# A graph-attention kernel whose first block gathers 27 columns instead of 38, with the edges left over fetched by one gather

## The chip, the cores and the metric

One core of one Trainium2 chip runs the whole kernel. The metric is the device time of one execution in microseconds (us). The kernel before takes 3907.3 us, the median of three runs (3907.01 to 3914.32).

## The reference

Three graph-attention layers over one graph of 6250 nodes, 100,000 edges and 256 features per node, all in float32. Edges are sorted by target. Cut to what matters:

```python
def gatv2(x, src, dst, Wl, Wr, att, b):          # 4 heads of 64, twice; self loops added
    xl, xr = (x @ Wl).reshape(n, 4, 64), (x @ Wr).reshape(n, 4, 64)
    e = leaky_relu(xl[src] + xr[dst], 0.2)
    logits = einsum('ehc,hc->eh', e, att)
    ex = exp(logits - segment_max(logits, dst)[dst])
    alpha = ex / segment_sum(ex, dst)[dst]
    return segment_sum(xl[src] * alpha[:, :, None], dst) + b

h = gatv2(elu(gatv2(x, ..., loops)), ..., loops)
x = layernorm(x + h)
# last layer: 8 heads of 32, no self loops
Wh = einsum('nf,hfd->hnd', x, W)
e = leaky_relu(s1[:, src] + s2[:, dst], 0.2)     # s1, s2: products of Wh with a
attn = softmax of e over the edges of each target
x = layernorm(x + segment_sum(attn * Wh[:, src], dst))
```

## The kernel before, in words

**Plan.** `make_plan` (0 to about 152 us) counts the edges of every node, puts the nodes in the order of their degrees, most edges first, and writes for every node a row with the numbers of its sources (`near_d`). The sorted nodes form 49 blocks of 128, one node to a partition. `columns()` fixes at build time, from the statistics of such a graph, how many source columns each block gets: 38, 25, 24, 23, 22, 21, 21, 20 and so on down to 9, together 814. Where the drawn graph does not fit these numbers, `fits` is zero and a general path of the kernel is taken instead. A node with fewer edges than its block has columns gets the number of an extra row ("nobody") in the places left over; its values make the softmax weight zero.

**Layers 0 and 1** (`layer2`, about 153 to 1492 and 1493 to 2728 us). For each block, `gather_rows` (L1207) issues one indirect DMA per column from GpSimd (POOL): 128 rows of about 1 KB, one to a partition, from a table in HBM (`xl_d`). The rows land in tiles `g` of up to nine columns; the pool `rows` has nine such tiles for all blocks. `row_tiles` and `chunks` cut a block into tiles of even size: with the node's own row as a further column, block 0 has 39 columns in five tiles, block 1 has 26 in three.

Each engine works in the order of the program, written by hand (`manual_schedule`). For block b the order is: load of block b+3 (`start`), gathers of block b+1, products for the own rows of block b+1 (`ready`), then `attend(b)`: on VectorE (DVE), tile by tile, `z` = max (L1396), `z` times the attention vector (L1397) and the sum per head into `lg` (L1398); the maximum `top` (L1272); on ScalarE (ACT) the exponentials `wt` with their sums `den` (L1279). Then `end(b-1)` on DVE: `h` = `acc` times `den` (L1415), and what follows from it. Then `weighted_sum(b)`: DVE multiplies the rows by their weights (L1309), ACT does so for a few of the last columns (L1308), and TensorE (PE) adds up the columns in PSUM, one product with the identity per column (L1316, `acc`). The next thing on DVE is the `z` of block b+1, while PE adds up the columns of block b. A tile of `rows` is free for a later gather when PE has read its columns.

In layer 0 the source numbers of blocks 0 to 2 are also sorted (`sort_sources`), so that 14, 12 and 11 of their gathers can be issued at the end of the layer before (`begin`, EARLY), ahead of the last four blocks of that layer's output.

**Last layer** (about 2729 to 3904 us). Gathers of blocks from `whs_d` without an own column (block 0: 38 columns in five tiles), the logits on DVE (L1567, L1571), exponentials on ACT (L1289), the weighted rows into one product tile `prod` of 27 columns (L1327) and their sum (L1336), all on DVE; PE has no part in it. The output is scattered by one indirect DMA per block (L1597).

Of the kernel before, what the change touches and what calls it, by code (L numbers as in the profile page):

```python
# [45 lines left out]
def columns(E, N, NB):  # L46

    mean = E / N
    pmf = [math.exp(-mean)]
    for k in range(1, 200):
        pmf.append(pmf[-1] * mean / k)
    over, sd = [], []
    for c in range(199):
        p = sum(pmf[c + 1 :])
        g = sum((k - mean) * pmf[k] for k in range(c + 1, 200))
        over.append(N * p)
        sd.append(math.sqrt(max(N * (p * (1.0 - p) - g * g / mean), 0.0)))  # L60
    cols = []
    for b in range(NB):
        most = P * b
        cols.append(next(
            c for c in range(199) if (over[c] + 3.5 * sd[c] <= most if b else over[c] < 0.01)
        ))
    low = max((c for c in range(199) if N - over[c] <= P // 4), default=0)
    high = next(c for c in range(199) if over[c] <= P // 4)
    return cols, low, high


@with_exitstack
# [565 lines left out]
@with_exitstack  # L638
def kernel(
    ctx: ExitStack,  # L640
    tc: tile.TileContext,
    x: bass.AP,
    src: bass.AP,
    dst: bass.AP,
    wl1: bass.AP,
    wr1: bass.AP,
    att1: bass.AP,
    b1: bass.AP,
    wl2: bass.AP,
    wr2: bass.AP,  # L650
    att2: bass.AP,
    b2: bass.AP,
    w3: bass.AP,
    a3: bass.AP,
    out: bass.AP,
):
    nc = tc.nc
    N, F = x.shape
    E = src.shape[0]
    NB = -(-N // P)  # L660
    NP = NB * P
    cols, low, high = columns(E, N, NB)
    CM = max(cols)
    H2, D2 = att1.shape
    H1 = w3.shape[0]
    W2 = H2 * (D2 + 1)

    dram = ctx.enter_context(tc.tile_pool(name="plan_dram", bufs=1, space=DRAM))
    plan = ctx.enter_context(tc.tile_pool(name="plan", bufs=1))
    node_i = plan.tile([P, NB], I32, name="node_i")  # L670
    fits = plan.tile([P, 1], I32, name="fits")
    done = plan.tile([P, 1], I32, name="done")
    ident = plan.tile([P, P], F32, name="ident")
    eps = plan.tile([P, 1], F32, name="eps")
    nobody = plan.tile([1, 2, max(W2 + 1, F + H1)], F32, name="nobody")
    att = [plan.tile([P, H2, D2 + 1], F32, name=f"att_r{i}") for i in range(2)]
    wc = [plan.tile([P, 2, 2, H2, D2 + 1], F32, name=f"wcat{i}") for i in range(2)]
    wh = plan.tile([P, 2, F + 2 * H1], F32, name="wh_cat")
    fixed = plan.tile([P, 4, F], F32, name="fixed_r")
    xl1_d = dram.tile([NP + 1, W2 + 1], F32, name="xl1_d")  # L680
    near_d = dram.tile([NP, CM + F], F32, name="near_d")

    with tc.manual_schedule():
        make_plan(
            tc, x, src, dst, ((wl1, wr1, att1), (wl2, wr2, att2)), (b1, b2), w3, a3,
            cols, low, high, node_i, fits, ident, eps, nobody, att, wc, wh, fixed, xl1_d, near_d,
        )
        nc.vector.memset(done, 0)

    att = [t.rearrange("p h d -> p (h d)") for t in att]  # L690
    wc = [w.rearrange("p j c h d -> p j c (h d)") for w in wc]
    ok = nc.values_load(fits[0:1, 0:1], min_val=0, max_val=1)
    with tc.If(ok != 0):
        with tc.manual_schedule():
            tile_by_degree(
                tc, x, att1, b1, b2, w3, a3, out, cols, node_i, near_d, ident, eps, nobody,
                xl1_d, att, wc, wh, fixed, done,
            )
    right = nc.values_load(done[0:1, 0:1], min_val=0, max_val=1)
    with tc.If(right == 0):  # L700
        tile_general_path(
            tc, x, src, dst, wl1, wr1, att1, b1, wl2, wr2, att2, b2, w3, a3, out,
        )
# [1 line left out]

@with_exitstack
def make_plan(
    ctx, tc, x, src, dst, layers, biases, w3, a3, cols, low, high, node_i, fits, ident, eps, nobody,
    att, wc, wh, fixed, xl1_d, near_d,
):  # L710

# [382 lines left out]
    nc.vector.tensor_scalar(  # L1094
        wrong[:, KE + NB :], upto[:, NB - 1 :], float(E), None, op0=OP.not_equal
    )
    bad = one.tile([P, 1], F32, name="bad")
    nc.vector.reduce_sum(bad, wrong, axis=AX.X)
    tables(4)
    pb = ps.tile([P, 1], F32, name="pb", tag="ph")  # L1100
    nc.tensor.matmul(pb, ones, bad, start=True, stop=True)
    nc.vector.tensor_scalar(fits, pb, 0.0, None, op0=OP.is_equal)
    right(0)
    left(1, nc.vector)
    right(1)
# [23 lines left out]
def tile_by_degree(  # L1129
# [9 lines left out]
    T = 9  # L1139
    A1 = F + H1  # L1140
    W2 = H2 * (D2 + 1)
    CM = max(cols)

    dram = ctx.enter_context(tc.tile_pool(name="deg_dram", bufs=1, space=DRAM))
    consts = ctx.enter_context(tc.tile_pool(name="deg_consts", bufs=1))
# [4 lines left out]
    def per_head(t, H):  # L1150
# [9 lines left out]


    AHEAD = (NB - LATE) * P
    KEY = CM.bit_length()
    assert (NP + 1) << KEY < 1 << 24
    CK = -(-CM // 8) * 8
    number = consts.tile([P, CK], F32, name="number")
    nc.gpsimd.iota(number, pattern=[[1, CK]], base=0, channel_multiplier=0,
                   allow_small_or_imprecise_dtypes=True)
    soon = consts.tile([P, len(EARLY), max(EARLY)], I32, name="soon")
    late = consts.tile([P, len(EARLY)], F32, name="late")  # L1170
    ones = consts.tile([P, P], F32, name="ones_l")
# [30 lines left out]
    def gather_rows(b, rows, cut, own, table, of, width, j0, j1):  # L1202


        for g, (s0, s1) in zip(rows, cut):
            for j in range(max(s0 - own, j0), min(s1 - own, j1)):
                nc.gpsimd.indirect_dma_start(  # L1207
                    out=g[:, j + own - s0, :width], out_offset=None, in_=table,
                    in_offset=source(of, b, j),
                )  # L1210

    def row_tiles(b, own):
        cut = chunks(cols[b] + own)
# [51 lines left out]
        cut = [n * i // k for i in range(k + 1)]  # L1265
        return list(zip(cut, cut[1:]))

    def weights(work, ps, lg, S, H, scalar=0):


        top = work.tile([P, H], F32, name="top")
        nc.vector.tensor_reduce(  # L1272
            top, lg[:, :S, :].rearrange("p s h -> p h s"), axis=AX.X, op=OP.max, negate=True
# [3 lines left out]
        if H <= 4:  # L1277
            for h in range(H):
                nc.scalar.activation(  # L1279
                    wt[:, :, h], lg[:, :S, h], AF.Exp, bias=top[:, h : h + 1],  # L1280
                    accum_out=den[:, h : h + 1],
                )
            by = None
            if scalar:
                by = work.tile([P, scalar, H], F32, name="by")
                nc.scalar.copy(by, wt[:, S - scalar :, :])
            return (wt, by), lambda: den
        nc.vector.tensor_add(lg[:, :S, :], lg[:, :S, :], top[:, None, :].to_broadcast([P, S, H]))
        nc.scalar.activation(wt, lg[:, :S, :], AF.Exp)  # L1289
# [4 lines left out]

        return (wt, None), add_up

    def weighted_sum(ps, rows, cut, wts, H, width, between):

        wt, by = wts
        acc = ps.tile([P, F], F32, name="acc")  # L1300
# [1 line left out]
        for g, (s0, s1) in zip(rows, cut):  # L1302
# [10 lines left out]
            if s0 == 0:  # L1313
                between()
            for t in range(n):
                nc.tensor.matmul(acc, ident, g4[:, t], start=s0 + t == 0, stop=s0 + t == S - 1)  # L1316
        return acc

    def added_up(work, prod, rows, cut, wts, H, width, between):
# [40 lines left out]
    def layer2(i, table, of, width, start, own, finish, follow):  # L1360
# [5 lines left out]
        with ExitStack() as es:  # L1366
# [9 lines left out]
            def gather(b):  # L1376
                first = EARLY[b] if b in begun else 0
                rows, cut = begun.pop(b) if first else row_tiles(b, 1)
                gather_rows(b, rows, cut, 1, table, of, width, first, cols[b])
                state[b] = [rows, cut]  # L1380

            later = []
# [6 lines left out]
            def attend(b):  # L1389
# [3 lines left out]
                for g, (s0, s1) in zip(rows, cut):  # L1393
# [4 lines left out]
                    nc.vector.reduce_sum(  # L1398
                        lg[:, s0:s1, :], z.rearrange("p t (h d) -> p t h d", h=H2), axis=AX.X
                    )  # L1400
                few = min(S // 3, cut[-1][1] - cut[-1][0] - 1) if b + 1 < NB else 0
                wt, new = weights(work, ps, lg, S, H2, few)
                while later:
                    later.pop()()
                if i == 0:
# [17 lines left out]
            for b in range(3):  # L1423
                if (i, b) not in loaded:
                    start(b)
            gather(0)
            ready(0)
            later.pop()()
# [3 lines left out]
            for b in range(NB):  # L1432
# [19 lines left out]
                    if b:  # L1452
                        last.append(rest())

                acc = weighted_sum(ps1, rows, cut, wt, H2, D2 + 1, between)
                if i == 0 and b + 1 < NB:
                    none(state[b + 1][2])
                if last:
# [92 lines left out]
    with ExitStack() as es:  # L1551
# [4 lines left out]
        def gather(b):  # L1556
            first = EARLY[b] if b in begun else 0
            rows, cut = begun.pop(b) if first else row_tiles(b, 0)
            gather_rows(b, rows, cut, 0, wh_d[:, :], spots, A1, first, cols[b])
            state[b] = (rows, cut)  # L1560

        def attend(b):
            rows, cut = state.pop(b)
            S = cols[b]
            lg = work.tile([P, CM, H1], F32, name="lg", bufs=2)
            for g, (s0, s1) in zip(rows, cut):
                nc.vector.tensor_add(  # L1567
                    lg[:, s0:s1, :], g[:, : s1 - s0, F:A1],
                    s2[:, b : b + 1, :].to_broadcast([P, s1 - s0, H1]),
                )  # L1570
# [3 lines left out]
            return rows, cut, *weights(work, ps, lg, S, H1)  # L1574

        def end(b, acc, den):
            h = work.tile([P, F], F32, name="h")
            nc.vector.tensor_mul(
                per_head(h, H1), per_head(acc, H1), den.unsqueeze(2).to_broadcast([P, H1, D1])
            )  # L1580
# [8 lines left out]
            return rest  # L1589

        gap = work.tile([P, 1], F32, name="gap", bufs=1)
        prod = work.tile([P, 3 * T, F], F32, name="weighted", bufs=1)

        def put_out(b, y, apart):
            if apart:
# [10 lines left out]
        for b in range(NB):  # L1606
# [12 lines left out]
                    puts[b - 1] = rest()  # L1619

            acc = added_up(work, prod, rows, cut, wt, H1, D1, between)
        puts[NB - 1] = end(NB - 1, acc, den)()
        for b in sorted(puts):
            put_out(*puts[b], apart=True)
# [28 lines left out]
```

## Time and profile before

| what | value |
|---|---|
| median of 3 runs | 3907.3 us (3907.01 to 3914.32) |
| the profiled execution | 3906.24 us; its span in the trace 3904.4 us |
| mean granted TensorE clock | 0.669 |
| DVE busy | 2859.7 us (73%) |
| POOL busy | 2558.8 us (66%) |
| PE busy | 1465.1 us (38%) |
| ACT busy | 1093.2 us (28%) |
| gathers per layer | 814, 0.95 us (layers 0 and 1) and 1.03 us (last layer) each |

The busy tenths of the page cut the span into 40 slices of 97.6 us. A row of the costliest groups has the line, the engine, the operation, the tiles written and read, the count, the busy time and the mean of one in ns, and then the idle time just before and what ended most of it. A row of the waits names who waited, for what, the total in us, how often and the longest. A line of the timeline has its start, its duration and, in brackets, the idle time before it.

### The profile page before, as it was taken

Reading aid. Unit: us, or ns where it says so; the run is one execution under the profiler, and the core shown is the slowest. Engines: PE = TensorE matmul, PEld = TensorE weight load, DVE = VectorE, ACT = ScalarE, POOL = GpSimd, SP = SyncE. Lnnn points to the kernel's source line nnn. Section 1 sums busy time; section 2 is a strip of 40 time slices with the busy share of each in tenths; the row PEclk is TensorE's granted clock in tenths of the full one; section 3 lists DMA queues with packets and bytes.
Section 4 is the critical chain, followed back from the end, with each engine's and each line's share of the span. In section 5 each row is a group of like instructions: output and inputs, shape, how many; then the busy total and the mean of one; then the engine's idle time right before and its main releaser. Section 6 shows DMA issues by size and latency. Waiting matters only on the chain.

```text
span 3904.4 us, 23669 instructions
## 1 busy us (share of the span) xinstructions
PE 1465.1 (38%) x5147; PEld 1100.0 (28%) x5147; DVE 2859.7 (73%) x2624; ACT 1093.2 (28%) x4179; POOL 2558.8 (66%) x2642
## 2 busy tenths in 40 slices
PE   5335655646667653355545455554000000000000
PEld 4223443435455542243433334442000000000000
DVE  6267888768888867798877889895686666666655
ACT  2123433434445441243334334442000000000000
POOL 6466666666666654666666666663777777777774
PEclk8667787777888886676766777776555555555555
DMA  8443333333334333333434344342433333333332
GB/s 192 101 94 100 104 103 100 105 102 103 105 103 107 104 102 71 103 106 105 112 104 111 107 110 111 109 111 69 100 107 105 97 96 97 97 97 96 97 97 56
DMA packets 197563, 399.62 MB, mean 102 GB/s; under 512 B 63516, under 2 KB 115994, under 8 KB 197396
## 3 DMA queue, kind: packets, MB, share of 16 engines
q0 software_dynamic: 123488, 342.06, 33.7%
q1 hardware_dynamic: 66226, 54.22, 4.9%
q10 hardware_dynamic: 7698, 1.74, 0.4%
q8 instruction: 45, 0.74, 0.1%
q14 instruction: 106, 0.87, 0.1%
HBM read 357.84 MB, written 40.42 MB: 102 GB/s over the span
## 4 chain that ended last, share of the span: by engine, by line
issue 24%; POOL 21%; PE 16%; DVE 14%; another core or an unknown queue 12%; ACT 9%; DMA 2%; DVEq 0%; SPq 0%; ACTq 0%; POOLq 0%
POOL g L1207 19%; PE acc L1316 10%; ACT g L1308 4%; PE pm L1261 3%; DVE z L1397 3%; DVE z L1396 3%; DVE lg L1398 3%; ACT wt L1279 2%; DVE weighted L1327 1%; DVE g L1309 1%; DMA g<-xl_d,near_r 1%; POOL out L1597 1%; ACT xT L1256 1%; PE pl L1261 1%
## 5 line engine op out<-in xcount | busy, mean ns | idle before, releaser
L1207 POOL DMA_INDIRECT g<-xl_d,near_r x1591 | 1508.6, 948 | 843.6 <-issue 455.7
L1316 PE MATMUL acc<-g,ident 128*128 128x256 f32 x3452 | 1015.0, 455 | 910.1 <-issue 361.4
L1316 PEld LDWEIGHTS acc<-g,ident 128*128 128x128 f32 x3452 | 768.0, 229 | 1152.9 <-issue 617.4
L1207 POOL DMA_INDIRECT g<-whs_d,near_r x777 | 802.2, 1032 | 293.9 <-issue 251.9
L1308 ACT ACTIVATE g<-g,by 128x64 f32<-128x64 f32 x2064 | 550.4, 337 | 331.3 <-issue 328.0
L1396 DVE TENSOR_TENSOR z<-g,pr 128x1820 f32<-128x1820 f32 (+4 forms) x236 | 503.4, 2133 | 39.3 <-DMA g<-xl_d,near_r 25.7
L1397 DVE TENSOR_TENSOR z<-z,at 128x1820 f32<-128x1820 f32 (+4 forms) x236 | 503.7, 2134 | 8.1
L1398 DVE TENSOR_REDUCE lg<-z 128x28 f32<-128x1820 f32 (+4 forms) x236 | 503.6, 2134 | 8.1
L1336 DVE TENSOR_REDUCE acc_v<-weighted 128x256 f32<-128x4096 f32 (+16 forms) x49 | 349.2, 7127 | 11.7 <-remote 6.1
L1309 DVE TENSOR_TENSOR g<-g,wt 128x1792 f32<-128x1792 f32 (+5 forms) x236 | 353.8, 1516 | 2.9
L1567 DVE TENSOR_TENSOR lg<-g,s_r 128x56 f32<-128x56 f32 (+4 forms) x113 | 22.8, 214 | 367.4 <-DMA g<-whs_d,near_r 300.0
L1289 ACT ACTIVATE wt<-lg 128x128 f32<-128x128 f32 (+17 forms) x49 | 14.0, 285 | 901.2 <-DVE top L1272 309.9
L1256 ACT COPY xT<-pt 128x256 f32<-128x256 f32 x147 | 55.0, 374 | 704.8 <-remote 367.3
L1327 DVE TENSOR_TENSOR weighted<-g,wt 128x1792 f32<-128x1792 f32 (+4 forms) x113 | 229.5, 2048 | 0.0
L1447 DVE RECIPROCAL den<-den 128x4 f32<-128x4 f32 x98 | 17.4, 177 | 226.8 <-ACT wt L1279 158.9
L1279 ACT ACTIVATE wt<-lg,top 128x19 f32<-128x19 f32 (+14 forms) x392 | 116.1, 296 | 209.0 <-DVE top L1272 83.7
L1415 DVE TENSOR_TENSOR h<-acc,den 128x256 f32<-128x256 f32 x98 | 40.7, 416 | 166.8 <-remote 122.3
L1261 PE MATMUL pm<-wh_cat,xT 128*128 128x272 f32 x196 | 83.9, 568 | 192.7 <-issue 108.7
L1261 PE MATMUL pm<-wcat,xT 128*128 128x260 f32 x392 | 138.5, 512 | 45.8 <-ACT xT L1256 44.8
L1261 PEld LDWEIGHTS pm<-wcat,xT 128*128 128x128 f32 x392 | 96.9, 261 | 82.1 <-ACT xT L1256 61.7
L1261 PEld LDWEIGHTS pm<-wh_cat,xT 128*128 128x128 f32 x196 | 46.0, 260 | 213.5 <-issue 113.5
L1597 POOL DMA_INDIRECT out<-y,node_i x49 | 50.3, 1027 | 49.6 <-ACT y L1358 35.6
(180 smaller groups left out, 1511.1 us busy)
## 6 DMA issues: line engine op xcount, KB each, us to landing
g<-xl_d,near_r POOLq DMA_INDIRECT x1591
g<-whs_d,near_r POOLq DMA_INDIRECT x777
whs_d<-row SPq DMA_DIRECT2D x49, 132.0 KB
xl_d<-xl SPq DMA_DIRECT2D x49, 130.0 KB
xl_d<-row SPq DMA_DIRECT2D x49, 130.0 KB
xr_d<-row SPq DMA_DIRECT2D x49, 130.0 KB
two<-xl_d SPq DMA_DIRECT2D x49, 130.0 KB
two<-xr_d SPq DMA_DIRECT2D x49, 130.0 KB
```

What stands on the lines that cost most here:

```text
L1207: nc.gpsimd.indirect_dma_start(out=g[:, j + own - s0, :width], out_offset=None, in_=table, in_offset=source(of, b, j),)
L1256: nc.scalar.copy(xT, pt)
L1261: nc.tensor.matmul(pm, xT[:, c, :], w[:, c, :], start=c == 0, stop=c == 1)
L1279: nc.scalar.activation(wt[:, :, h], lg[:, :S, h], AF.Exp, bias=top[:, h : h + 1], accum_out=den[:, h : h + 1],)
L1308: nc.scalar.mul(g4[:, t, h, :], g4[:, t, h, :], by[:, t - m, h : h + 1])
L1309: nc.vector.tensor_mul(g4[:, :m], g4[:, :m], wt[:, s0 : s0 + m, :].unsqueeze(3).to_broadcast([P, m, H, F // H]),)
L1316: nc.tensor.matmul(acc, ident, g4[:, t], start=s0 + t == 0, stop=s0 + t == S - 1)
L1327: nc.vector.tensor_mul(prod[:, s0 - base : s1 - base, :].rearrange("p t (h d) -> p t h d", h=H), g[:, :n, :F].rearrange("p t (h d) -> p t ...
L1336: nc.vector.reduce_sum(part, prod[:, : s1 - base, :].rearrange("p s f -> p f s"), axis=AX.X)
L1396: nc.vector.tensor_max(z, g[:, :n, :W2], xr[:, None, :].to_broadcast([P, n, W2]))
L1397: nc.vector.tensor_mul(z, z, at[:, None, :].to_broadcast([P, n, W2]))
L1398: nc.vector.reduce_sum(lg[:, s0:s1, :], z.rearrange("p t (h d) -> p t h d", h=H2), axis=AX.X)
```

## The change

Block 0 gets `held` = 27 columns instead of 38. Its nodes with more than 27 edges have "other" edges; `held` is chosen such that their number over the block is at most 128 (by the same statistics; the plan counts them and otherwise takes the general path). `find_few` gives each of them a partition, once, at the beginning of layer 0: `node_of` and `edges_of` are 0/1 matrices between nodes and edges, `hot` marks which of its node's other edges an edge is, `few_at` is its source number. In each layer `gather_few` fetches the rows of all of them with one gather, after the gathers of block 0. In layers 0 and 1 their logits are worked out edge by edge (the node's own values come to the edges by a product with `node_of`), and go to their nodes by a product with `edges_of` (`few_logits`); `top`, `wt` and `den` then cover 27 + 1 + 11 places. `few_sum` takes the weights back to the edges by a product with `node_of`, multiplies the rows, and adds them to the nodes with a product with `edges_of`, into the same `acc` as the columns and after them. In the last layer the same two functions work on a PSUM tile of their own, added to `acc_v`. The sort of sources has 32 keys instead of 40, `h` of the last layer has two buffers instead of three and `prod` 24 columns instead of 27.

```diff
@@ columns
+    pmf += [0.0] * 200
+    held = next(
+        c for c in range(199)
+        if N * sum((k - c) * pmf[k] for k in range(c, 200))
+        + 3.5 * math.sqrt(N * sum((k - c) ** 2 * pmf[k] for k in range(c, 200))) <= P
+    )
@@ make_plan
+    nc.vector.tensor_scalar(
+        bad[:, 1:], got[:, 2, :1], -float(held), 0.0, op0=OP.add, op1=OP.max
+    )
...
-    nc.vector.tensor_scalar(fits, pb, 0.0, None, op0=OP.is_equal)
+    many = one.tile([P, 1], F32, name="many")
+    nc.vector.tensor_scalar(many, pb[:, 1:], float(P), None, op0=OP.is_gt)
+    nc.vector.tensor_add(many, many, pb[:, :1])
+    nc.vector.tensor_scalar(fits, many, 0.0, None, op0=OP.is_equal)
@@ tile_by_degree (called with [held] + cols[1:])
+    CM = near_d.shape[1] - F
+    FEW = CM - cols[0]
...
+    def find_few(work, ps):
+        got = work.tile([P, 1 + FEW], F32, name="few_got", bufs=1)
+        nc.vector.tensor_copy(got[:, 1:], sources[:, 0, cols[0] :])
+        nc.vector.tensor_single_scalar(lack, got[:, 1:], float(NP), op=OP.is_lt)
...
+        po = ps.tile([P, 1], F32, name="few_o", tag="tp")
+        nc.tensor.matmul(po, edges_of, n[:, :1], start=True, stop=True)
...
+        pk = ps.tile([P, 1 + FEW], F32, name="few_k", tag="tp")
+        nc.tensor.matmul(pk, node_of, got, start=True, stop=True)
...
+        nc.vector.tensor_copy(few_at[:, :1], which)
+        pe = ps.tile([P, P], F32, name="few_e", tag="tp")
+        nc.tensor.transpose(pe, node_of, ident)
+        nc.scalar.copy(edges_of, pe)
+
+    def gather_few(table, j, width):
+        nc.gpsimd.indirect_dma_start(
+            out=few_row[:, :width], out_offset=None, in_=table,
+            in_offset=bass.IndirectOffsetOnAxis(ap=few_at[:, j : j + 1], axis=0),
+        )
+
+    def few_logits(work, ps, lg, few, H):
+        each = work.tile([P, FEW, H], F32, name="few_each", bufs=1)
+        nc.vector.tensor_mul(each, few (broadcast), hot (broadcast))
+        pf = ps.tile([P, FEW, H], F32, name="few_lg", tag="tp")
+        nc.tensor.matmul(pf, edges_of, each, start=True, stop=True)
+        nc.vector.tensor_add(lg[the FEW places], pf, lack (broadcast))
+
+    def few_sum(work, ps, acc, wt, S, H, width, first):
+        share = work.tile([P, FEW, H], F32, name="few_each", bufs=1)
+        nc.scalar.copy(share, wt[:, S : S + FEW, :])
+        pw = ps.tile([P, FEW, H], F32, name="few_w", tag="tp")
+        nc.tensor.matmul(pw, node_of, share, start=True, stop=True)
+        each = work.tile([P, FEW, H], F32, name="few_weight", bufs=1)
+        nc.vector.tensor_mul(each, pw, hot (broadcast))
+        weight = work.tile([P, H], F32, name="few_wt", bufs=1)
+        nc.vector.reduce_sum(weight, each, axis=AX.X)
+        part = work.tile([P, F], F32, name="few_part", bufs=1)
+        nc.vector.tensor_mul(part, few_row, weight (broadcast))
+        nc.tensor.matmul(acc, edges_of, part, start=first, stop=True)
@@ weighted_sum
             for t in range(n):
-                nc.tensor.matmul(acc, ident, g4[:, t], start=s0 + t == 0, stop=s0 + t == S - 1)
+                nc.tensor.matmul(
+                    acc, ident, g4[:, t], start=s0 + t == 0, stop=s0 + t == S - 1 and not more
+                )
+        if more:
+            more(acc, wt, S)
         return acc
@@ layer2, gather
                 gather_rows(b, rows, cut, 1, table, of, width, first, cols[b])
+                if b == 0:
+                    gather_few(table, i, width)
@@ layer2, attend, after the tiles' z
+                if b == 0:
+                    own_r = work.tile([P, W2], F32, name="few_own", bufs=1)
+                    nc.scalar.copy(own_r, xr)
+                    po = pst.tile([P, W2], F32, name="few_r", tag="tp")
+                    nc.tensor.matmul(po, node_of, own_r, start=True, stop=True)
+                    none(po)
+                    z = zp.tile([P, T, W2], F32, name="z")[:, 0, :]
+                    nc.vector.tensor_max(z, few_row[:, :W2], po)
+                    nc.vector.tensor_mul(z, z, at)
+                    few_lg = work.tile([P, H2], F32, name="few_lg", bufs=1)
+                    nc.vector.reduce_sum(few_lg, per_head(z, H2), axis=AX.X)
+                    few_logits(work, pst, lg, few_lg, H2)
+                    if i == 0:
+                        nc.vector.tensor_copy(few_at[:, 1:], few_row[:, W2 : W2 + 1])
@@ layer2, before gather(0)
+            if i == 0:
+                find_few(work, pst)
@@ layer2, per block
-                acc = weighted_sum(ps1, rows, cut, wt, H2, D2 + 1, between)
+                acc = weighted_sum(
+                    ps1, rows, cut, wt, H2, D2 + 1, between,
+                    b == 0 and (lambda acc, wt, S: few_sum(
+                        work, pst, acc, wt, S, H2, D2 + 1, False)),
+                )
@@ last layer
+            if b == 0:
+                gather_few(wh_d[:, :], 1, A1)
...
+            if b == 0:
+                few_logits(work, ps, lg, few_row[:, F:A1], H1)
+                nc.vector.tensor_add(lg[the FEW places], lg[the FEW places], s2 of block 0 (broadcast))
...
-        prod = work.tile([P, 3 * T, F], F32, name="weighted", bufs=1)
+        prod = work.tile([P, 24, F], F32, name="weighted", bufs=1)
...
             acc = added_up(work, prod, rows, cut, wt, H1, D1, between)
+            if b == 0:
+                more = ps.tile([P, F], F32, name="few_acc", tag="tp")
+                few_sum(work, ps, more, wt[0], cols[0], H1, D1, True)
+                nc.vector.tensor_add(acc, acc, more)
```

Views of tiles are shortened in the diff: "(broadcast)" stands for the repetition over heads or places.

## The prediction
> **What bounds the kernel now.** I read the page first: busy tenths, then the costliest groups, then the waits, then the timelines of the stretches that the change touches.
>
> ```profile
> PE   5335655646667653355545455554000000000000
> DVE  6267888768888867798877889895686666666655
> POOL 6466666666666654666666666663777777777774
> ...
> L1207 POOL DMA_INDIRECT g<-xl_d,near_r x1591 | 1508.6, 948 | 843.6 <-issue 455.7
> L1316 PE MATMUL acc<-g,ident 128*128 128x256 f32 x3452 | 1015.0, 455 | 910.1 <-issue 361.4
> ...
> L1207 POOL DMA_INDIRECT g<-whs_d,near_r x777 | 802.2, 1032 | 293.9 <-issue 251.9
> ```
>
> No engine is full, but POOL is level all through: it issues one gather per column and does nothing else. A gather is busy 0.948 us and, in the timeline, comes 0.30 us after the last: a pitch of 1.25 us. In the last layer, issues and output scatters (797 from 2771 to 3857) follow without a stall, 1.363 us apart: that layer is POOL's. In layers 0 and 1 POOL stalls once a block:
>
> ```profile
> POOL g L1207 <- remote: 151.2, 43, 6.1
> ...
> DVE h L1415 <- remote: 122.3, 11, 27.0
> ...
> POOL g L1207 <- PE acc L1316: 93.6, 39, 19.4
> POOL g L1207 <- ACT g L1308: 88.1, 23, 4.7
> ```
>
> These are waits for one of the nine `rows` tiles to come free, which `acc` (PE) decides. So there the cycle is gathers plus one wait, and it holds DVE too (`h`, once 27 us). The starts of the two layers show how PE answers:
>
> ```profile
> 222.75 11.24 PE L1316 MATMUL acc<-g,ident 128*128 128x256 f32 x44 [58.79 <-issue]
> 236.95 0.58 PE L1316 MATMUL acc<-g,ident 128*128 128x256 f32 x1 [2.96 <-issue]
> ...
> 268.45 7.66 PE L1316 MATMUL acc<-g,ident 128*128 128x256 f32 x22 [1.51 <-issue]
> ```
> ```profile
> 276.15 0.42 DVE L1415 TENSOR_TENSOR h<-acc,den 128x256 f32<-128x256 f32 x1 [16.55 <-PE acc L1316]
> ```
> ```profile
> 1540.28 8.94 DVE L1309 TENSOR_TENSOR g<-g,wt 128x1792 f32<-128x1792 f32 x5
> 1549.14 2.31 DVE L1396 TENSOR_TENSOR z<-g,pr 128x2080 f32<-128x2080 f32 x1
> ...
> 1599.30 0.42 DVE L1415 TENSOR_TENSOR h<-acc,den 128x256 f32<-128x256 f32 x1 [27.02 <-remote]
> ```
> ```profile
> 1527.70 0.95 POOL L1207 DMA_INDIRECT g<-xl_d,near_r  x1 [0.30 <-issue]
> 1548.06 0.94 POOL L1207 DMA_INDIRECT g<-xl_d,near_r  x1 [19.41 <-PE acc L1316]
> ...
> 1593.07 0.95 POOL L1207 DMA_INDIRECT g<-xl_d,near_r  x1 [0.31 <-issue]
> 1599.54 0.94 POOL L1207 DMA_INDIRECT g<-xl_d,near_r  x1 [5.52 <-remote]
> ```
>
> In layer 0, PE takes 22 columns in 11 us (two records a column), then, while POOL issues without a pause (156.9 to 256.7), one record every 2.1 to 3.5 us, and at 268, with POOL idle, the last 11 columns in 7.7 us. In layer 1 PE ends block 0's columns at about 1562, but `h` starts only at 1599.3, five us after POOL fell silent at 1594. I read from this, without knowing why, that PE's progress reaches others late while POOL issues a long run.
>
> [...] the 27.02 us idle before `h` has later DVE work behind it. [...] in layer 1 a gather takes 0.94 to 0.95 us both under DVE's `z` work (1549 to 1572) and with DVE idle (1572 to 1594). [...] Here DVE waits 6.5 us from the last gather's end (204.4 to 210.99)[...]. [...]
>
> **The change, part by part.** The sum is made against the profiled execution, 3906.24 us (span 3904.4, 1.8 around it), 1.1 below the median 3907.3. In the inputs, 49 edges lie beyond the 27th of their node (of 32 at most), so the new path is taken.
>
> *Issues.* 11 gathers less and one more per layer: -10 x 1.25 = -12.5 us on POOL, three times (-37.5).
>
> *Plan and find_few.* Three more DVE operations of about 0.18 us and wider iotas: +0.5. find_few, some 15 small DVE operations and three PE products, is 5 to 15 us, hidden: DVE has no column of block 0 before about 166 and slack until 175, and its result is needed when POOL has issued 27 gathers (190). Cost 0; without that cover, at most 15.
>
> *Head of layers 0 and 1.* `top` of block 0 is at 218.05 and 1537.61. Its last gather comes 13.75 earlier; the landing, with less padding, 6.5 to about 3 us (-3.5; 0 at worst); the last chunk is 7 columns, not 8, three operations (-0.7). New on DVE: max, mul, reduce at 0.42, three of 0.18 and a hop to PE and back at some 1.5 (2.03 is what `den` waits for ACT here): +3.3. Together -14.7: `top` at 203.4 and 1522.9. The few gather, 1.25 behind, lands while the last chunk is worked. The sort's missing round is 3 x 0.5, beside the wait.
>
> *few_sum, the new wait.* `weighted_sum` (block 0) ends with a product on PE behind all 28 columns, and DVE's multiply of it stands ahead of block 1's `z` (22.8 us up to its `top`, 1549.14 to 1571.95), which until now ran under PE's work. Queued behind it on DVE: `z`, the sort, `h` and the multiplies of block 1; ACT's exponentials of block 1 wait for its `top`, PE's columns of block 1 for the multiplies, and POOL in turn for block 1's tiles. SP and its stores have nothing in the queue but `h`'s rows. few_sum itself: 0.18+0.18+0.42 on DVE, two PE hops: 2 to 4 us.
>
> In **layer 1**, POOL runs 14+13+4 gathers (1493.9 to 1532.7), then stalls as now. The multiplies end at 1533, PE starts about 1527 with POOL silent from 1532.7 until the first tile is free. 28 columns at 0.49 us (19.25 us for 39) end about 1541 to 1550; few_sum to 1544 to 1553, `z` to 1567 to 1576, and `h` then does not have to wait: 1567 to 1581 against 1599.30. Taken: -23 (-18 to -32; +9 if PE's product is held until the end of POOL's second run).
>
> In **layer 0**, POOL runs on from 156.9: 28, 25 and up to 25 issues, so it falls silent at about 257 to 267. PE starts about 208, takes 22 columns by 219, and the other 6 and the product crawl as now (14 records x 2.5 = 35 us: 254) or wait for the silence. DVE resumes at 258 to 283; + 23 + 7 for the sort: `h` at 290 to 310 against 276.15. But POOL, 12.5 us ahead and with two to three tiles more in hand, starts block 4 (318.3 now) at 303 to 318. So of the -12.5 a part is lost: taken -5 (-14 to +12; +34 if POOL's cycle does not absorb DVE's lateness). At the layer's end the 37 early gathers for layer 1 stay, but with tiles of seven columns block 0's 14 (and its own row) touch three tiles instead of two; of nine tiles that makes seven instead of six, so POOL falls silent some gathers earlier and the last blocks may see PE's progress earlier: -4 to 0, taken -2.
>
> *Last layer.* Now 24+25 gathers to block 3's first, with a stall of 6.91 at 2770.86 (block 0's first tile); the new 14+13+13 need nine tiles and none back. -10 issues at 1.25 to 1.39, and the stall mostly gone but for a later one: -17 (-13 to -21). few_logits and few_sum, 5 to 10 us on DVE, replace 11 columns of multiply and add (0.29+0.45 us each = 8.1): 0. DVE is full for the first 62 us (61.3 of 62), but 63% busy after (648.6 of 1027), so it regains 10 us within 30. The new wait, of the first logits for the few gather, costs 0: it lands 7 us or less after its issue (2746), while DVE is idle (5.7 us busy of 42 from 2729 to 2771); without that cover it would be the 6.5 us of a landing. `prod` of 24 columns cuts block 1's 25 into two sums and an add (0.42+0.2): under the same slack. `h` in two buffers: a block's `h` is used up before the next but one starts; 0.
>
> Sum: 0.5-5-2-23-17 = -46.5: **3860** against 3906.2, 3861 beside the median.
>
> **Rivals.** *Only the issues count*: the head starts melt in stalls on the way and each layer gives 12.5 to 13.9: -38 to -41, about 3867. For: outside the heads period per gather is even (1.375). Inside my range. *Only the last layer gains*: few_sum's wait eats the heads of both others: -17, about 3890. For: the crawl in layer 0. *Slower*: DVE stopped at few_sum (layers 0 and 1), its price the `z` work (22.8 us) taken out of PE's shadow. It decides from the point at which PE's product is seen later than the 16.6 (layer 0) and 27.0 (layer 1) us that `h` waits now can pay for. Then +34, +9 and only -10 in the last layer: +33, about 3940. Against: in layer 1 POOL does fall silent for 19 us just there. *Not what it says* (more than 128 edges left over, general path): excluded by the 49.
>
> **How the numbers follow.** 0.2% is 7.8 us, about what a measurement can tell from no change. My forecast 0.5, issues only 0.24, last layer only 0.12 (half of it reaching towards no change), slower 0.11, the rest between. Faster 0.84, same 0.05, slower 0.11. Range: forecast's best ends (-14, -4, -32, -21: 3836) to the last-layer case with a lost head (3897).
>
> **What would show it.** 814 gathers become 804 per layer. Right: `h` of block 0 in layer 1 some 20 us nearer to the layer's first gather, DVE idle ahead of few_sum's multiply by 8 to 17 us there and by 45 to 70 in layer 0; POOL's 19.41 stall about 5; the last layer 17 shorter with no early stall. Wrong: few_sum's wait in layer 1 past 30 us, or block 4's first gather in layer 0 later than now.

## The result, and the profile after

The changed kernel takes 3876.4 us (median of 6 runs, 3867.9 to 3887.2) against 3907.2 us (6 runs, 3901.8 to 3917.7): ratio 0.9917, 95% interval 0.9896 to 0.9939. That is 31 us faster, where 46 had been forecast (3861, range 3836 to 3897). The span of its profiled execution is 3878.7 us, 25.7 less than before.

The page of the changed kernel, busy tenths and costliest groups:

```profile
PE   6324665556667763355544545554000000000000
...
DVE  6228988668888876899876988896676565666665
...
POOL 6464666666666645666666666664777777777774
...
L1235 POOL DMA_INDIRECT g<-xl_d,near_r x1569 | 1487.4, 948 | 858.7 <-issue 454.3
L1418 PE MATMUL acc<-g,ident 128*128 128x256 f32 x3408 | 1015.9, 461 | 765.3 <-issue 282.7
...
L1235 POOL DMA_INDIRECT g<-whs_d,near_r x766 | 793.2, 1036 | 284.2 <-issue 250.0
```

The gathers are as many fewer as they should be (22 and 11; the gathers into `few_row` are counted apart), and each takes as long as before (0.948 us, and 1.036 against 1.032 in the last layer). But DVE's third slice (194 to 291 us), at 6 tenths before, is down to 2: that is the start of layer 0. The waits name it:

```profile
POOL g L1235 <- PE acc L1418: 131.7, 50, 16.0
POOL g L1235 <- remote: 115.5, 37, 4.3
...
DVE few_weight L1303 <- remote: 86.3, 2, 68.7
```

The new wait, DVE's multiply in few_sum for the product of PE, is 86.3 us in two instances, one of 68.7. The stages of the two profiled executions, in us, cut by POOL's timeline at the first load and at each later layer's first late gather (the first that was not issued ahead, at the end of the layer before):

| stage | before | after | difference | forecast |
|---|---|---|---|---|
| layer 0 (first load to layer 1's first late gather) | 1340.8 | 1361.6 | +20.9 | -7 |
| layer 1 (to the last layer's first late gather) | 1235.3 | 1210.0 | -25.3 | -23 |
| last layer (to the end) | 1175.1 | 1156.3 | -18.8 | -17 |

The first load itself came 2.4 us earlier. So two stages did as forecast, and layer 0 went the other way. Its start, on PE and on DVE (timelines; idle time before each line in brackets):

```profile
204.06 12.63 PE L1418 MATMUL acc<-g,ident 128*128 128x256 f32 x44 [4.97 <-issue]
219.81 0.59 PE L1418 MATMUL acc<-g,ident 128*128 128x256 f32 x1 [3.11 <-issue]
...
249.91 0.59 PE L1418 MATMUL acc<-g,ident 128*128 128x256 f32 x1 [2.91 <-issue]
...
254.81 0.23 PE L1298 MATMUL few_w<-few_each,node_of 128*128 128x44 f32 x1 [2.57 <-issue]
```
```profile
201.99 6.21 DVE L1411 TENSOR_TENSOR g<-g,wt 128x1792 f32<-128x1792 f32 x4
276.95 0.20 DVE L1303 TENSOR_TENSOR few_weight<-few_w,few_hot 128x44 f32<-128x44 f32 x1 [68.75 <-remote]
...
278.04 2.32 DVE L1504 TENSOR_TENSOR z<-g,pr 128x2080 f32<-128x2080 f32 x1
...
304.12 0.41 DVE L1537 TENSOR_TENSOR h<-acc,den 128x256 f32<-128x256 f32 x1
```

22 columns go through PE in 12.6 us, the last six at one record per 1.4 to 3.5 us (two records a column), and the product that DVE needs has its last record at 254.8. DVE goes on at 276.95, 22 us after that record and 9.5 us after the end of POOL's last gather (267.5). Only then comes block 1's `z`. Before, it followed the multiplies of block 0 at once:

```profile
220.67 8.95 DVE L1309 TENSOR_TENSOR g<-g,wt 128x1792 f32<-128x1792 f32 x5
...
229.78 2.32 DVE L1396 TENSOR_TENSOR z<-g,pr 128x2080 f32<-128x2080 f32 x1
```

The start of layer 1 on POOL, for comparison with the 19.41 us stall of before:

```profile
1549.88 0.95 POOL L1235 DMA_INDIRECT g<-xl_d,near_r  x1 [0.30 <-issue]
1556.04 0.94 POOL L1235 DMA_INDIRECT g<-xl_d,near_r  x1 [5.22 <-PE acc L1418]
```

In the last layer POOL issues from 2722.4 to 3192 without a stall of 2 us; the 6.91 us one is gone.

### The profile page after: what moved, and what is told of

Same layout as the page of the kernel before. It is cut to its first block, busy times and chain, and to the rows that moved or that the text cites. A ratio compares the mean times of both kernels' runs of the same rounds, so it can differ in the third digit from the quotient of the medians.

```text
span 3878.7 us, 23608 instructions
## 1 busy us (share of the span) xinstructions
PE 1481.8 (38%) x5130; PEld 1113.8 (29%) x5130; DVE 2836.2 (73%) x2648; ACT 1091.1 (28%) x4176; POOL 2530.5 (65%) x2613
## 4 chain that ended last, share of the span: by engine, by line
issue 20%; POOL 20%; DVE 13%; PE 10%; another core or an unknown queue 6%; ACT 5%; DMA 1%; DVEq 0%; POOLq 0%; ACTq 0%
POOL g L1235 18%; PE acc L1418 6%; DVE z L1505 4%; DVE z L1504 4%; DVE lg L1506 3%; PE pm L1362 3%; ACT g L1410 2%; ACT wt L1381 2%; DVE g L1411 1%; POOL out L1733 1%; DMA g<-xl_d,near_r 1%; DVE weighted L1433 1%; ACT xT L1357 0%; PE pt L1355 0%
## 5 line engine op out<-in xcount | busy, mean ns | idle before, releaser
L1235 POOL DMA_INDIRECT g<-xl_d,near_r x1569 | 1487.4, 948 | 858.7 <-issue 454.3
L1235 POOL DMA_INDIRECT g<-whs_d,near_r x766 | 793.2, 1036 | 284.2 <-issue 250.0
L1442 DVE TENSOR_REDUCE acc_v<-weighted 128x256 f32<-128x4096 f32 (+15 forms) x49 | 343.7, 7014 | 16.5 <-remote 8.3
L1411 DVE TENSOR_TENSOR g<-g,wt 128x1792 f32<-128x1792 f32 (+8 forms) x234 | 348.4, 1505 | 2.9
L1362 PE MATMUL pm<-wh_cat,xT 128*128 128x272 f32 x196 | 77.5, 531 | 183.8 <-ACT xT L1357 95.5
L1362 PEld LDWEIGHTS pm<-wcat,xT 128*128 128x128 f32 x392 | 94.8, 255 | 90.5 <-ACT xT L1357 64.6
L1362 PE MATMUL pl<-wcat,xT 128*128 128x260 f32 x196 | 64.0, 455 | 55.5 <-issue 40.4
```

What stands on the lines that cost most here:

```text
L1235: nc.gpsimd.indirect_dma_start(out=g[:, j + own - s0, :width], out_offset=None, in_=table, in_offset=source(of, b, j),)
L1362: nc.tensor.matmul(pm, xT[:, c, :], w[:, c, :], start=c == 0, stop=c == 1)
L1411: nc.vector.tensor_mul(g4[:, :m], g4[:, :m], wt[:, s0 : s0 + m, :].unsqueeze(3).to_broadcast([P, m, H, F // H]),)
L1442: nc.vector.reduce_sum(part, prod[:, : s1 - base, :].rearrange("p s f -> p f s"), axis=AX.X)
```

## The experiments

The runs went to several chips, and these are of two kinds. On some the kernel before takes 3907 to 3921 us, and in layer 0 PE is slow and seen late while POOL issues (changed kernel, e12: a record per 1.4 to 3.5 us, waits of 68.75 and 68.27 us at few_sum); on others it takes 3406 to 3412 us, and PE is not (e7: 30 records in 6.64 us, a wait of 10.00 us). The kinds differ in more than that: the last layer, in which PE has no part (no record from 2729 on), takes 1175.1 us before on the first and 1067.9 on the second (e8). The prediction and the comparison above are from the first kind, as are e1 to e4, e11 and e12; e5 to e10 ran on the second. Every ratio is against the kernel before on the same chip, with its 95% interval; the lengths of layers are those of one execution of each. The theories: **A**, layer 0's loss is the place of few_sum, with DVE standing in front of block 1's `z`; **B**, it comes from stalls elsewhere in the layer. Later, on why PE's product comes so late: **P**, because POOL issues a long run; **Q**, for reasons of PE's own. Diffs are shortened.

### e1: few_sum after block 1's z work, in both layers

```diff
-  b == 0 and (lambda acc, wt, S: few_sum(work, pst, acc, wt, S, H2, D2 + 1, False))
+  b == 0 and (lambda acc, wt, S: kept_few.append((acc, wt, S)))
...
   rows, cut, wt, new = attend(b)
+  if kept_few:
+      few_sum(work, pst, *kept_few.pop(), H2, D2 + 1, False)
   if b:
       rest = end(b - 1, acc, den)
```

> few_sum of block 0 is called in layers 0 and 1 only after attend of block 1, so that DVE does block 1's z work while PE adds up block 0's columns; nothing else differs from the changed kernel. Theory A (in layer 0 the change lost its gain because DVE stood 68.8 us at few_sum's first multiply with block 1's z work behind it): layer 0 is 15 to 25 us shorter than in the changed kernel; in layer 1, where POOL fell silent early anyway, the last product now comes into POOL's next run (1556 to 1596) and h waits for its end: 0 to +10. Together 3853 to 3866. Theory B (layer 0 lost its time in stalls that have nothing to do with few_sum's place, such as those at its end): within 5 us of the changed kernel, 3871 to 3881.

Measured: 3844.3 us against 3910.0, ratio 0.9825 (0.9798 to 0.9853). Layer 0 is 7.1 us shorter than before, so 27.9 shorter than in the changed kernel: theory A, and more than the 15 to 25 it had said (the total is below its 3853 to 3866). In layer 1 the forecast of a later `h` was wrong: `h` of block 0 comes 64.6 us after the first late gather, against 77.5 in the changed kernel and 105.4 before. PE had block 0's columns done by 1537.3, and POOL had paused before its second run (1529.5 to 1534.75).

### e2: the same in layer 0 only

```diff
-  b == 0 and (lambda acc, wt, S: few_sum(work, pst, acc, wt, S, H2, D2 + 1, False))
+  b == 0 and ((lambda acc, wt, S: kept_few.append((acc, wt, S))) if i == 0 else
+              (lambda acc, wt, S: few_sum(work, pst, acc, wt, S, H2, D2 + 1, False)))
```

> few_sum of block 0 is called after attend of block 1 in layer 0 only; layer 1 as in the changed kernel. Theory A: h of block 0 in layer 0 at about 279 instead of 304.1, the first gather of block 6 at about 375 instead of 392, the layer 15 to 25 us shorter, the total 3851 to 3861, at or below the kernel with both moved. Theory B: within 5 us of the changed kernel.

Measured: 3841.9 us, ratio 0.9837 (0.9797 to 0.9878), not to be told from e1 and again below the expected 3851 to 3861. The timeline of DVE in layer 0:

```profile
212.83 2.32 DVE L1504 TENSOR_TENSOR z<-g,pr 128x2080 f32<-128x2080 f32 x1
...
286.01 0.20 DVE L1303 TENSOR_TENSOR few_weight<-few_w,few_hot 128x44 f32<-128x44 f32 x1 [45.47 <-PE few_w L1298]
...
288.25 0.42 DVE L1537 TENSOR_TENSOR h<-acc,den 128x256 f32<-128x256 f32 x1 [1.31 <-issue]
```

From the first load on (155.1 here, 150.8 in the changed kernel) the product is seen 4.7 us later than there, so the expected `h` at 279 was missed, and DVE still waits 45 us. But the 27.7 us of `z` and sort (212.83 to 240.54) are done ahead of it, and `h` is 20 us earlier. The product is as late as it was; what stands behind the wait has changed. Block 6's first gather is at 371.23 (about 375 expected, 392.01 in the changed kernel). At `h` of block 9, from the first load on, e1 and e2 agree: 13.1 and 12.9 us earlier than before. By the end of the layer they differ by 14.7 us, with the same code in it (7.1 and 21.8 us shorter than before), and layer 1, here the same as in the changed kernel, is some 10 us shorter than there: so much can two traces differ by themselves.

### e3: 27 columns, the other edges left out

```diff
-                if b == 0:
-                    gather_few(table, i, width)
...
-                    few_logits(work, pst, lg, few_lg, H2)
...
-                wt, new = weights(work, ps, lg, S if b else S + FEW, H2, few, S)
+                wt, new = weights(work, ps, lg, S, H2, few, S)
...
-            if i == 0:
-                find_few(work, pst)
...
-                    b == 0 and (lambda acc, wt, S: few_sum(
-                        work, pst, acc, wt, S, H2, D2 + 1, False)),
+                    None,
...
-            S = cols[b] if b else CM
+            S = cols[b]
```

> Block 0 has 27 columns and the other 49 edges are left out of the computation (no find_few, no 28th gather, no few_logits, no few_sum). It gives what the missing issues alone are worth, with no wait added. Theory A: layer 0 12 to 20 us shorter than before instead of 18.5 longer, layer 1 20 to 28 shorter, last layer 19 to 21 shorter: 3840 to 3856. Theory B: layer 0 is again longer than before or unchanged, so 3868 to 3880.

Measured: 3845.4 us, ratio 0.9837 (0.9806 to 0.9868). Layer 0 is 11.1 us shorter than before, layer 1 32.0, the last 20.8 (12 to 20, 20 to 28 and 19 to 21 expected). So the work on the other edges (find_few, the 28th gather, the products) costs nothing that can be seen beside e1, which does all of it.

### e4: the kernel before with the wait alone

```diff
   acc = weighted_sum(ps1, rows, cut, wt, H2, D2 + 1, between)
+  if b == 0:
+      seen = work.tile([P, 1], F32, name="seen", bufs=1)
+      nc.vector.tensor_copy(seen, acc[:, :1])
```

> The kernel before with 38 columns, and one DVE copy of a single column of acc after weighted_sum of block 0 in layers 0 and 1: the wait alone, 0.2 us of work. Theory A: in layer 0 DVE stands until about 276 and h of block 0 moves from 276 to 305, the layer gets 10 to 28 us longer; in layer 1 block 1's z work begins when PE's 39 columns are seen, 0 to +10; total 3917 to 3945. Theory B: within 5 us of the kernel before.

Measured: 3934.5 us, 24.5 slower, ratio 1.0057 (1.0033 to 1.0081). In layer 0, timeline of DVE:

```profile
276.61 0.16 DVE L1458 COPY seen<-acc 128x1 f32<-128x1 f32 x1 [46.09 <-PE acc L1316]
...
307.68 0.41 DVE L1415 TENSOR_TENSOR h<-acc,den 128x256 f32<-128x256 f32 x1
```

A copy of 0.16 us makes layer 0 17.3 us longer and layer 1 9.5 us. The wait alone has the cost: A is shown from both sides, by taking `z` out from behind the wait (e1, e2) and by adding the wait to a kernel without few_sum.

### e5, e9, e11: POOL waits in layer 0 before block 2's gathers

The tile is `part` of few_sum, kept in `parts`.

```diff
+  if b == 1 and i == 0:
+      quiet = work.tile([P, 1], F32, name="quiet", bufs=1)
+      nc.gpsimd.tensor_copy(quiet, parts[-1][:, :1])
   if b + 1 < NB:
       gather(b + 1)
```

> The changed kernel, with one more POOL operation in layer 0: ahead of block 2's gathers POOL copies one column of few_part, and so issues nothing from the end of block 1's gathers (about 223) until few_sum's DVE part is done. Theory P (PE's progress is held up and seen late because POOL issues a long run): PE ends block 0's columns at once when POOL falls silent, few_sum's first multiply is at 228 to 237 instead of 276.95, h of block 0 at 256 to 268 instead of 304.1, layer 0 20 to 35 us shorter than in the changed kernel although POOL is kept waiting, total 3843 to 3858. Theory Q (PE takes 2 to 3 us a record there for reasons of its own[...]): few_sum's multiply at 250 to 256, POOL loses some 30 us of issue, layer 0 as long or longer, total 3872 to 3900.

> As e5: the changed kernel, and POOL waits in layer 0 ahead of block 2's gathers until few_part is there. On a chip with before at about 3906 us, theory P (PE's progress is held up and seen late because POOL issues a long run): few_sum's multiply at 228 to 237 instead of 276.95, h of block 0 at 256 to 268 instead of 304.1, layer 0 20 to 35 us shorter than in the changed kernel, total 3843 to 3858. Theory Q (PE is slow there for reasons of its own): the multiply at 250 to 256, layer 0 as long or longer, total 3872 to 3900. On a chip with before at about 3406 us: 0.987 to 0.990 of before, as e5.

> As e5 and e9, for a chip on which the kernel before takes about 3906 us. There theory P (PE's progress is held up and seen late because POOL issues a long run): few_sum's first multiply at 225 to 237 instead of 276.95, h of block 0 at 256 to 268, layer 0 20 to 35 us shorter than in the changed kernel beside it (e12). Theory Q (PE is slow there for reasons of its own): the multiply at 250 to 256 and layer 0 as long or longer. On a chip with before at about 3406 us: 0.987 to 0.990 of before, a third time.

On the second kind of chip the pause changes nothing that the comparison can tell: e5 3366.5 us, 0.9888 (0.9872 to 0.9905), e9 3373.7 us, 0.9885 (0.9869 to 0.9902), beside 0.9889 of the changed kernel (e7). There few_sum waited only 10 to 11 us in any case (10.00 in e7, 11.28 in e5). On the first kind, e11: 3861.1 us, 0.9852 (0.9822 to 0.9882), beside e12 3884.2 us on the same chip. Its timelines of PE and DVE in layer 0:

```profile
236.85 0.58 PE L1420 MATMUL acc<-g,ident 128*128 128x256 f32 x1 [2.21 <-ACT few_each L1297]
238.25 3.42 PE L1420 MATMUL acc<-g,ident 128*128 128x256 f32 x7 [0.82 <-issue]
241.47 0.49 PE L1299 MATMUL few_w<-few_each,node_of 128*128 128x44 f32 x2
```
```profile
242.00 0.20 DVE L1304 TENSOR_TENSOR few_weight<-few_w,few_hot 128x44 f32<-128x44 f32 x1 [26.49 <-PE few_w L1299]
```

POOL is silent from 230. Until 237 PE still takes a record per 2 to 3 us, then seven in 3.4 us, and DVE has the product 0.04 us after its last record; in the changed kernel that took 22 us. The multiply is at 242 and `h` of block 0 at 269.17: five and one us behind P's latest values, in an execution whose first load came 7.0 us later than in the changed kernel's, and the multiply is ahead of Q's 250. Layer 0 is 33.3 us shorter than in e12 (1333.5 against 1366.8), although POOL stood 13 us in it: P. The granted clock does not explain the gaps either: in the changed kernel it is 0.50 from 220 to 260, and there a record takes 0.58 to 0.59 us, while the records are 1.4 to 3.5 us apart. Whether it is POOL's issuing or the transfers that it starts, e11 cannot tell: the pause stops both.

### e6: block 0 in five tiles

```diff
   cut = chunks(cols[b] + own)
+  if b == 0 and own:
+      n = cols[0] + 1
+      cut = [n * i // 5 for i in range(6)]
+      cut = list(zip(cut, cut[1:]))
```

> The changed kernel with block 0's 28 columns in five tiles of 5 or 6 instead of four of 7 in layers 0 and 1: as many tiles as before the change, as few gathers as after it. Theory T (in layer 1 the gain over the 12.5 us of issues comes from the tile that is left in POOL's hand at the layer's start): POOL's stall at the layer's start is back at about 12 to 19 us instead of 5.2, layer 1 is 5 to 12 us longer than in the changed kernel. Theory I (it comes from the issues and from DVE's shorter block 0): layer 1 within 4 us of the changed kernel up to h of block 5. Both: total 3866 to 3890.

It ran on the second kind of chip: 3364.9 us, 0.9883 (0.9866 to 0.9899), as e7. The stall at layer 1's start is back:

```profile
1285.24 0.94 POOL L1235 DMA_INDIRECT g<-xl_d,near_r  x1 [13.67 <-PE acc L1422]
```

In e7 there is none there, and before (e8) it is 20.52 us. So the tile in hand does decide that stall, as T said; but layer 1 is no longer for it (1069.6 us, 1071.7 in e7). On these chips DVE is busy for 975 of 1025 us of the layer (e7), which would explain that. What the stall costs where POOL sets the pace was not tried.

### e7, e12: the changed kernel again; e8: the kernel before; e10: few_sum late, again

> The changed kernel once more, unaltered, for a second trace of it: what of its layer 0 (20.9 us longer than before from the first load on) comes again. Theory A: few_sum's wait of about 69 us and h of block 0 some 30 us behind the layer's start of before come again, and the layer is 10 to 22 us longer than before; the stalls in the middle and at the end of the layers differ by up to 8 us from the first trace. Theory B: the head comes again, but the layer as a whole is no longer than before. Total 3868 to 3885.

> The changed kernel once more beside e11. On a chip with before at about 3906 us: few_sum's wait in layer 0 again 60 to 75 us, 0.988 to 0.995 of before. On a chip with before at about 3406 us: that wait 10 us, 0.987 to 0.990.

> The kernel before, unaltered, for a trace of it on the chip of the next two. On a chip on which it takes about 3906 us: POOL's stalls of 3 to 5 us per block and the waits of 16 to 27 us ahead of h of block 0 come again. On a chip on which it takes about 3406 us: no such stalls (PE's products are seen at once there), h of block 0 follows its columns within 3 us, and each of the three stages is 12 to 14 us longer than in the changed kernel (e7): there the issues and the columns are all that the change is worth.

> As e1: few_sum after attend of block 1 in layers 0 and 1. On a chip with before at about 3906 us: again 0.980 to 0.986 of before. On a chip with before at about 3406 us few_sum's multiply waited only 10 us (e7), so DVE gains 10 us in each of the two layers at most: 0.982 to 0.987 of before if DVE sets the pace there, 0.988 to 0.990 if POOL does.

On the first kind of chip e12 (3884.2 us, 0.9900, 0.9869 to 0.9930) repeats the loss: few_sum waits 68.27 us, layer 0 takes 1366.8 us, layer 1 1207.1, the last 1156.6 (+26.0, -28.3 and -18.5 beside the trace of before). On the second kind, where the expectation of a long wait in e7 did not hold, e7 takes 3367.6 us, 0.9889 (0.9873 to 0.9906). The timeline of its DVE in layer 0:

```profile
196.58 0.20 DVE L1303 TENSOR_TENSOR few_weight<-few_w,few_hot 128x44 f32<-128x44 f32 x1 [10.00 <-PE few_w L1298]
```

And of PE in the kernel before there (e8, one run of 3416.4 us; the runs beside it have a median of 3412.3):

```profile
204.10 20.00 PE L1316 MATMUL acc<-g,ident 128*128 128x256 f32 x78 [59.27 <-DVE g L1309]
```

All 39 columns in 20 us, under the same train of gathers. There the change gains in all three stages, cut as in the table above: -12.6 us in layer 0, -7.0 in layer 1, -24.3 in the last (e7 against e8, on two chips; 12 to 14 had been expected of each). e10: 3357.1 us, 0.9841 (0.9824 to 0.9857); its layers 0 and 1 are 5.2 and 7.7 us shorter than in e7, so few_sum's place is worth something there as well.

## Why the prediction was right or wrong

**Right**: what bounds the layers, and most steps.

- Issues: ten fewer per layer at 1.25 us. Where no wait was added (e3), `h` of block 9 in layer 0 is 15.2 us earlier from the first load on, in e1 13.1, against 12.5 worked out.
- Head: `top` of block 0 in layer 0 (199.37) comes 48.6 us after the first load, against 64.9 before: -16.3 (forecast -14.7). The last columns of block 0 are there 2.5 us after their gather's end (188.0 to 190.49; 6.5 before; the 3 taken was the author's estimate, and that less padding does it is not shown). The few logits took DVE 2.7 us with their hop (196.71 to 199.37; 3.3 taken).
- few_sum's multiply in layer 0 at 276.95 (258 to 283) and `h` at 304.12 (290 to 310); block 4's first gather at 314.24 (303 to 318).
- Layer 1: -25.3 (-23). POOL's stall is 5.22 instead of 19.41, -14.2, and the issues -12.5. DVE waited 17.55 us at few_sum, just over the 8 to 17 given. The same code gave -35.0 in e2, so the close fit is in part luck.
- Last layer: -18.8 (-17), with no stall at the start; few_logits and few_sum there cost some 2 us (e3, without them, -20.8).

**Wrong**: the term for layer 0, "taken -5 (-14 to +12; +34 if POOL's cycle does not absorb DVE's lateness)", with -2 for its end; it was +20.9, beyond the +12. Each event at the head fell where it was worked out; the step that failed is the one from there to the layer. Block 4's first gather was taken for what the layer keeps. But POOL had reached it on tiles in hand, while DVE was 28 us late, and then paid twice (timeline of POOL, after and before):

```profile
314.24 0.95 POOL L1235 DMA_INDIRECT g<-xl_d,near_r  x1 [15.96 <-PE acc L1418]
...
351.42 0.94 POOL L1235 DMA_INDIRECT g<-xl_d,near_r  x1 [8.73 <-DVE z L1505]
...
392.01 0.94 POOL L1235 DMA_INDIRECT g<-xl_d,near_r  x1 [13.39 <-DVE z L1505]
```
```profile
351.40 0.95 POOL L1207 DMA_INDIRECT g<-xl_d,near_r  x1 [4.62 <-ACT g L1308]
...
383.31 0.94 POOL L1207 DMA_INDIRECT g<-xl_d,near_r  x1 [4.68 <-ACT g L1308]
```

The last two stalls are 8.73 and 13.39 instead of 4.62 and 4.68. From the first load on, `h` of block 9 is 11.0 us later than before (12.9 in e12), so the head is worth 11 to 13 us of loss instead of 5 of gain. The rest of the +20.9 comes later in the layer, in stalls that differ from run to run: after block 9 the layer differs from that of before by -9 us (e2) to +13 us (e12), with the same code in e1 (+6) and e2 (-9) there. Which part of it is the change's could not be told apart. The wait at the layer's end was taken as -2; it isn't visible in this scatter. Neither of the two signs of being wrong came (17.55 us in layer 1, not past 30; block 4's first gather at 314.24, not later than 318.3): both look at points ahead of the step that failed.

So the slower rival's mechanism was the true one in layer 0, at some six tenths of its price (20.9 of 34), and the rest of that rival (+9 in layer 1, only -10 in the last) did not happen. The forecast held because the two other stages came as worked out, and because its range was wide enough for one lost head: layer 0 alone missed its term by 28 us. Some smaller slips did not matter: the upper end of the range, 3897, is given without a sum; in the last layer 24 + 26 gathers, not 24 + 25, stood ahead of block 3's; and the even 1.375 us per gather outside the heads, given for the rival of the issues alone, fits the last layer (1.371) but not layers 0 and 1 (1.54 from 318 to 1400 us, 1.46 from 1640 to 2650). That DVE takes its work in the order of the program shows in the traces: in the changed kernel it is idle for 68.75 us with block 1's `z` behind the wait, and that `z` starts at 278.04; with `z` ahead of the wait (e2) it starts at 212.83. On why PE's progress is late, e11 shows that POOL's run of gathers does it on one kind of chip; e8 shows that the same run does not on another. By what path is open.

The version that beats both kernels on both kinds of chip is e1: 0.9825 on the one, 0.9841 (e10) on the other.

## What to carry to other kernels

Before an engine that takes its work in the order of the program (DVE here, idle for 68.75 us with `z` behind it) is made to wait for another's result, see which of its later instructions do not need that result, and put those first: here the wait itself stayed (45 us in e2) and cost nothing that can be measured (ratio 0.9837, as in e3 without the wait). A train of transfers that runs ahead on buffers in hand can hide such a lateness for a few blocks and then charge it, as here (block 4's first gather on time at 314.24, then stalls of 8.73 and 13.39 us), so the first points that come on time prove little; follow the lateness until the buffers are used up. The saving at POOL's issue rate came in full at the head of layer 0 where no wait was added (e3: 15.2 us by `h` of block 9, 12.5 worked out), and in layer 1 (25.3 us shorter), where the new wait takes the place of an old one: few_sum's 17.55 us in layer 1 replaced a wait of 27.02, its 68.75 in layer 0 one of 16.55.

## What the runs showed of the hardware

On the chips on which the kernel before takes 3907 to 3921 us, PE slows down in layer 0 while POOL issues gathers without a pause: in the changed kernel it has 44 records in 12.63 us (0.29 us each), then one per 1.4 to 3.5 us, and its product is seen 9.5 us after the end of POOL's last gather (the same in e12). In layer 1 of the kernel before it does not: 78 records take 19.25 us (1542.35 to 1561.60), though POOL issues again from 1548.06. On the other chips PE takes 78 records in 20.0 us under the same issue (e8), and the same kernel takes 3412 us. A pause of POOL (e11) brings the slow PE back to 0.49 us a record within 9 us (POOL silent from 229.95, seven records in 3.42 us from 238.25).

PE is not alone in this. ACT's multiplies slow down in the same stretch (timeline of ACT, changed kernel):

```profile
202.87 1.78 ACT L1410 ACTIVATE g<-g,by 128x64 f32<-128x64 f32 x7
...
219.09 0.35 ACT L1410 ACTIVATE g<-g,by 128x64 f32<-128x64 f32 x1 [1.05 <-issue]
220.49 0.35 ACT L1410 ACTIVATE g<-g,by 128x64 f32<-128x64 f32 x1 [1.05 <-issue]
```

Seven took 1.78 us, then they start 1.40 us apart; at the start of layer 1 of the kernel before, with POOL silent until 1548.06, 28 take 6.79 us (1540.45 to 1547.24). Those of the changed kernel do not hold PE up: the last ends at 226.45, PE's last column at 250.5. Between 221 and 256 all 31 starts of PE, of its weight loads and of ACT lie within 0.02 us of one grid of 0.70 us (so do PE's 14 in e12 from 223.95 to 258.95); POOL's, 1.25 us apart, do not. That points to something that PE and ACT share, rather than PE's own speed; what it is, no run here shows. Nor is it shown how much of the 500 us between the two kinds of chip comes from it: in the last layer, whose columns do not go through PE, a gather of the changed kernel takes POOL 1.036 us on the one kind and 0.950 on the other (e7).
